# A graph network layer: the first product in one 16-bit pass per tile, with 30 moving nodes

## The chip, the core and the metric

The kernel runs on one core of a Trainium2 chip. The metric is the device time of one execution in microseconds (us), the median of several runs. A core has five engines with queues of their own: TensorE (matmuls; PE in the profile, its weight loads PEld), VectorE (DVE), ScalarE (ACT), GpSimd (POOL) and SyncE (SP), which here only issues transfers. Transfers run on 16 DMA engines.

## The reference

N = 6250 nodes with H = 128 features, E = 100000 edges sorted by destination, four attributes an edge. What is computed, cut to what matters:

```python
src, dst = edge_index                       # dst is sorted
msg_in = concat([x[src], x[dst], edge_attr], axis=1)      # E x 260
h = silu(msg_in @ mW1 + mb1)                              # E x 128
messages = h @ mW2 + mb2
aggregated = segment_sum(messages, dst, num_segments=N)   # N x 128
u = silu(concat([x, aggregated], axis=1) @ uW1 + ub1)
updated = u @ uW2 + ub2
x1 = layer_norm(x + updated, ln_g, ln_b)
out = layernorm(x + x1)
```

Inputs and outputs are float32.

## The kernel before

**Splitting mW1.** `msg_in @ mW1` is the sum of three terms: A[src], with A = x @ mW1[:128]; B[dst], with B = x @ mW1[128:256] + mb1; and the attributes times the last four rows, We. A and B are made once per node (`make_a`, `make_b`) and written to the tables tab_a and tab_b in DRAM. A row of A is fetched for every edge; B, as dst is sorted, is needed only for a short range of nodes at a time.

**Tiles and groups.** An edge tile is 128 edges, a group is G = 8 tiles, so there are NG = 98 groups. Every fifth group from 15 to 90 (16 groups, `by_sort`) does without gathers: A of its edges is selected by 16-bit products with 0/1 matrices (`select`, tile po). The other 82 groups are `listed`; for each, POOL issues eight indirect transfers (`fetch`, line 234, tile ga), of 128 rows each.

**A listed group** goes through these steps:

- `load` (lines 578 to 585), on SP's queue: near, the group's 1024 destinations broadcast to 80 partitions (line 435, 320 KB); mv[:80], 80 consecutive rows of B from the group's first destination on (line 584, 40 KB); and the group's attributes into rows 80 to 83 of st (line 585). We lies in rows 80 to 83 of mv for good.
- `matrices`, on VectorE: st[:80] is the 0/1 matrix "edge e has node base + p" (line 593, a comparison whose accumulator also gives each node's count of edges); oh is the same matrix with the edges on the partitions, 80 columns for each tile (line 603).
- `before_rows`, on TensorE: pre = st.T @ mv, for each tile 128 edges by 128 features, which is B[dst] plus the attributes' term. Everything is float32.
- `hidden`: VectorE adds pre to the gathered rows (line 645), ScalarE takes SiLU (line 646) into h.
- `sums`, on TensorE: pt += h.T @ oh over the eight tiles, so 128 features by 80 nodes, with oh padded to WS = 112 columns. The counts of four groups are transposed together at every fourth group.
- `add`, on VectorE: pt into acc at the group's offset (line 692) and the counts into deg (line 686).

mW2 is merged with uW1, so acc and deg feed the node work directly (`node_u`, `node_y`, `node_z`, `node_o`, once per batch of four node tiles).

**Order.** The order is written out by hand: one stage per listed group g, in which the engines get, in this order, attributes, work on a sorted group, the gathers of the fourth listed group ahead, `load` of the third, `matrices` of the second, `before_rows` and `hidden` of the next, then `sums` and `add` of g, then the rest of the sorted work and the node work (`node_stage`, where `make_b` of later batches ends the stage). Each engine takes its instructions in that order. Every second gather also waits for a product some three stages back, chosen by a running count of TensorE's work (`counted`, with a `share` for cheap products).

**Buffers.** pre has two PSUM buffers (`wide`), which alternate; pt (`narrow`), pn (`bank`) and po (`selected`) have one each. There are four buffers for mv, three for st, two for near.

**Opening and guard.** Before the stages, `tables` turns x, makes A for all nodes and B for the first batches, and prepares lists; the sorting for the 16 groups runs on VectorE during the first stages. Range checks over the indices end in `bad_i`; a slow general path follows only if it is set.

Of the kernel before, what the change touches and what calls it, by code (L numbers as in the profile page):

```python
# [21 lines left out]
P = 128  # L22
# [5 lines left out]
def kernel(  # L28
# [28 lines left out]
    W = 80  # L57
    WS = 112
    NW = NP + W
    AW = 768  # L60
    K1 = W + ED
# [146 lines left out]
    w_row_i = first.tile([P, W], I32, name="w_row_i")  # L208
    nc.gpsimd.iota(w_row_i, pattern=[[1, W]], base=0, channel_multiplier=0)
# [13 lines left out]
    tab_b = dram.tile([NW, H], F32, name="tab_b")  # L223
    sd = dram.tile([4, QN * GE], F16, name="sd")
    ea_d = dram.tile([ED, NG * GE], F32, name="ea_d")
# [3 lines left out]
    def fetch(g):  # L229
# [20 lines left out]
        ceil_i, pattern=[[BN * P, NB + 1], [0, G]], base=BN * P - W, channel_multiplier=0  # L250
    )
    pos_i = first.tile([R, P], I32, name="pos_i")
# [9 lines left out]
    if rest:  # L262
        nc.vector.memset(dst_l[low:NG], N)
    nc.sync.dma_start(dst_l[:low], dst[: low * GE].rearrange("(p j) -> p j", j=GE))
# [9 lines left out]
    w_row = ps1.tile([P, W], F32, name="w_row")  # L274
# [17 lines left out]
    deg_s = []  # L292
    for k in range(3):
        deg_s.append(consts.tile([W, P], F32, name=f"deg_s{k}"))
        nc.vector.memset(deg_s[k], 0.0)

    def deg_at(g):
        s, i = divmod(g - 1, 4) if g else (-1, 0)
        return deg_s[(s + 1) % 3], 32 * i

    def deg_col(g):
        t, c = deg_at(g)
        return t[:, c : c + 1]
# [19 lines left out]
    def lists_1():  # L323
        base_c = first.tile([NG, 1], F32, name="base_c")
        nc.vector.tensor_copy(base_c, dst_l[:, 0:1])
        rel_n = first.tile([P, GE], F32, name="rel_n")[:NG]
        nc.vector.tensor_scalar(rel_n, dst_l, base_c, None, op0=OP.subtract)
        parts.update(base_c=base_c, rel_n=rel_n)
        nc.vector.memset(floor_i[:, 0:1], 0)
        nc.vector.memset(floor_i[:, last[NB - 2] + 1 :], batches[NB - 1][0] * P)  # L330
        nc.vector.memset(ceil_i[:, 84 + G // 2 :], batches[NB - 1][0] * P - W)
        nc.vector.memset(ceil_i[:, 92 + G // 2 :], NP)
        for g in range(NG):
            k = made_for(g)
            usual = (g + G // 2) // G
            if k < usual and g >= G:
                nc.vector.memset(
                    ceil_i[:, g + G // 2 : g + G // 2 + 1],
                    sum(n for _, n in batches[: k + 1]) * P - W,
                )  # L340

    def lists_2():
# [12 lines left out]
        nc.vector.tensor_copy(base_f, to_row(parts["base_c"], NG))  # L355
        parts["base_f"] = base_f

    def lists_3():
# [3 lines left out]
        nc.vector.tensor_scalar(base_p, p_b[:, :NG], p_col, None, op0=OP.add)  # L362
# [6 lines left out]
        nc.vector.tensor_tensor(base_i, base_f, lim, op=OP.min)  # L369
# [12 lines left out]
    mid = (W - 1) / 2  # L382

    def check_1():
        parts["far"] = first.tile([NG, 2], F32, name="far")
        nc.vector.tensor_reduce(parts["far"][:, 0:1], parts["rel_n"], AX.X, OP.max)

    def check_2():
        far = parts["far"]
        nc.vector.tensor_reduce(far[:, 1:2], parts["rel_n"], AX.X, OP.min)  # L390
# [33 lines left out]
    def attribute_rows(c):  # L424
        t = turn.tile([EQ, ED, EJ], F32, name="ea_t")
        nc.scalar.copy(t, ea_l.pop(c).rearrange("q (j d) -> q d j", d=ED))
        to = ea_d[:, c * EC : (c + 1) * EC]
        nc.scalar.dma_start(to.rearrange("d (q j) -> q d j", q=EQ), t)

    def destinations(g):  # L430
        near[g] = work.tile([P, GE], I32, name="near")[:W]
        n = min(GE, E - g * GE)
        if n < GE:
            nc.vector.memset(near[g][:, n:], N)
        nc.sync.dma_start(
            near[g][:, :n],
            dst[g * GE : g * GE + n].rearrange("(o e) -> o e", o=1).to_broadcast([W, n]),
        )
# [18 lines left out]
    def make_b(k):  # L457
        i0, n = batches[k]
        pm = bank()
        product(k, 1, pm)  # L460
        tb = node.tile([P, BN, H], F32, name="o")
        nc.vector.tensor_add(tb[:, :n], pm[:, :n], b1[:, None, :].to_broadcast([P, n, H]))
        nc.sync.dma_start(by_node(tab_b)[:, i0 : i0 + n, :], tb[:, :n])
# [33 lines left out]
    for k in range(NM):  # L497
        mv.append(consts.tile([P, H], F32, name=f"mv{k}"))

    def fill_mv(t):  # L500
        nc.vector.memset(t[P // 2 :], 0.0)
        nc.sync.dma_start(t[W:K1], mW1[2 * H :])

    def fill_ends():
        zeros = first.tile([W, H], F32, name="zeros")
        nc.vector.memset(zeros, 0.0)
        nc.sync.dma_start(tab_b[NP:NW], zeros)
        pad = first.tile([ED, NG * GE - E], F32, name="pad")
# [42 lines left out]
    for k in range(NST):  # L551
        stbuf.append(consts.tile([P, GE], F32, name=f"st{k}"))
    ohbuf = []
    for k in range(NST + 1):
        ohbuf.append(kept.tile([P, G, WS], F32, name=f"oh{k}"))

    fills = [lambda t=t: fill_mv(t) for t in mv] + [fill_ends]
    fills += [lambda t=t: nc.vector.memset(t[:, :, W:], 0.0) for t in ohbuf]
    fills += [lambda t=t: nc.vector.memset(t[P // 2 :], 0.0) for t in stbuf]
# [6 lines left out]
    def load_bases(g):  # L566
        for to, of, eng, top in ((bases, base_i, ENG.SP, NP), (offs, off_i, ENG.DVE, AW - W)):
# [10 lines left out]
    def load(g):  # L578
# [5 lines left out]
        nc.sync.dma_start(mv[turn_of(g) % NM][:W], tab_b[bass.ds(bases[g], W), :])  # L584
        nc.sync.dma_start(stbuf[turn_of(g) % NST][W:K1], ea_d[:, g * GE : (g + 1) * GE])

    oh, pre, xg, h_s = {}, {}, {}, {}

    def matrices(g):
        if g >= NG:  # L590
            return
        n = tiles_of(g)
# [927 lines left out]
```

## Time and profile before

| | |
|---|---|
| median of 3 runs | 1078.12 us (1074.33 to 1084.27) |
| profiled execution, its own time | 1078.25 us |
| span of the profile | 1076.5 us |
| mean granted TensorE clock | 0.863 |
| first gather starts / last gather starts | 4.93 / 1045.23 us |
| 205 to 1045 us: TensorE busy, granted clock | 664.5 of 840 us, 0.89 |
| the same stretch: VectorE, ScalarE, GpSimd busy | 424.7, 341.0, 511.8 us |
| DMA moved | 108.94 MB, of it near 81 x 320 KB, mv 82 x 40 KB, st 82 x 16 KB |

How to read it: a line of a group gives the line of the source, engine, operation, output<-inputs, shape and count; then, after the first bar, the busy time in us and the mean of one in ns; after the second, the idle time of the engine just before them and what ended it. The chain of waits is followed back from the last instruction; its shares say which work set the end. Line 148 is the helper that records every matmul, so products are told apart by their tiles.

### The profile page before, as it was taken

To read this page: it belongs to the slowest core of one execution; us is meant where nothing else is said; L and a number is where in the kernel's file an instruction comes from. 1 tells how busy PE (TensorE), PEld (TensorE's weight loads), DVE (VectorE), ACT (ScalarE), POOL (GpSimd) and SP (SyncE) were. 2 spreads that over 40 slices of the span, in tenths; PEclk is the share of its full clock that TensorE was granted. 3 is DMA by queue.
4 is the path that set the end of the run, shared out by engine and by line. 5 is a ranking of instruction groups with operands and counts; after the bars stand their busy time and mean duration, and the time that the engine had idled before them with its cause. 6 is when DMAs were issued, how large, how long until landed. Compare 5 with 4: busy or idle time off the path is not lost.

```text
span 1076.5 us, 17905 instructions
## 1 busy us (share of the span) xinstructions
PE 807.8 (75%) x6479; PEld 687.8 (64%) x6479; DVE 558.1 (52%) x1357; ACT 404.1 (38%) x543; POOL 641.9 (60%) x665
## 2 busy tenths in 40 slices
PE   5548557668878788877877878777878877877874
PEld 4548455566757576666776666666577666676653
DVE  3463677843555283555373555444374445473282
ACT  1122114533343354344344353343253344363142
POOL 6646557765656666565666566556566566666550
PEclk8778779789888989798998989879879788999795
DMA  9544315342424252525163443424343434242220
GB/s 231 140 114 117 93 57 143 87 101 81 114 85 116 72 137 76 121 75 131 57 152 84 117 109 97 110 80 100 87 112 93 99 92 120 71 111 81 85 77 25
DMA packets 86890, 108.94 MB, mean 101 GB/s; under 512 B 22348, under 2 KB 63456, under 8 KB 86794
## 3 DMA queue, kind: packets, MB, share of 16 engines
q1 hardware_dynamic: 52498, 58.26, 21.3%
q0 software_dynamic: 20928, 42.90, 15.2%
q10 hardware_dynamic: 13368, 6.56, 2.3%
q8 instruction: 53, 0.87, 0.4%
q14 instruction: 43, 0.35, 0.1%
HBM read 96.26 MB, written 11.40 MB: 100 GB/s over the span
## 4 chain that ended last, share of the span: by engine, by line
PE 52%; issue 16%; DVE 13%; another core or an unknown queue 7%; ACT 5%; DMA 3%; POOL 2%; SPq 1%; DVEq 0%; ACTq 0%; POOLq 0%
PE pt L148 14%; PE po L148 14%; PE pre L148 13%; PE pn L148 8%; PE pn L151 2%; POOL ga L234 2%; DMA ga<-tab_a,src_i 1%; DVE st L593 1%; DVE oh L603 1%; ACT h L646 1%; DVE ga L645 1%; ACT O L1027 1%; PE pre L151 1%; DVE O L1023 1%
## 5 line engine op out<-in xcount | busy, mean ns | idle before, releaser
L234 POOL DMA_INDIRECT ga<-tab_a,src_i x614 | 601.9, 980 | 380.4 <-issue 202.4
L148 PE MATMUL pre<-mv,st 128*128 128x128 f32 x1308 | 202.3, 310 | 27.4 <-issue 12.8
L148 PEld LDWEIGHTS pre<-mv,st 128*128 128x128 f32 x1308 | 190.5, 225 | 40.3 <-issue 29.2
L148 PE MATMUL pt<-oh,h 128*128 128x112 f32 x1308 | 191.5, 305 | 25.6 <-issue 12.6
L148 PEld LDWEIGHTS pt<-oh,h 128*128 128x128 f32 x1308 | 180.1, 218 | 39.5 <-issue 24.3
L646 ACT ACTIVATE h<-ga 128x1024 f32<-128x1024 f32 (+1 forms) x78 | 81.1, 1042 | 317.7 <-DVE ga L645 222.6
L692 DVE TENSOR_TENSOR acc<-acc,pt 128x80 f32 x98 | 23.3, 238 | 341.3 <-PE pt L148 104.1
L148 PE MATMUL po<-O,A_low 128*128 128x157 bf16 (+47 forms) x896 | 163.8, 225 | 22.3 <-issue 22.3
L148 PE MATMUL po<-O,A 128*128 128x156 bf16 (+37 forms) x1376 | 140.2, 227 | 36.6 <-issue 33.0
L148 PEld LDWEIGHTS <-A 128*128 128x128 bf16 x1376 | 112.4, 104 | 58.3 <-issue 57.3
L645 DVE TENSOR_TENSOR ga<-ga,pre 128x1024 f32<-128x1024 f32 (+1 forms) x78 | 93.3, 1197 | 54.7 <-PE po L148 22.0
L593 DVE TENSOR_SCALAR_CACHE_REDUCE st<-near,base_p 80x1024 f32<-80x1024 int32 x82 | 103.4, 1261 | 11.9 <-issue 10.4
L148 PEld LDWEIGHTS <-A_low 128*128 128x128 bf16 x896 | 91.0, 103 | 20.6 <-issue 20.3
L1027 ACT ACTIVATE O<-sc,p_less 128x512 bf16<-128x512 f16 x128 | 84.8, 711 | 1.4 <-DMA sc<-sd 1.4
L1028 ACT ACTIVATE O<-O,ones 128x1024 bf16<-128x1024 bf16 x64 | 73.5, 1148 | 2.1
L603 DVE TENSOR_TENSOR oh<-w_row,rel 128x640 f32<-128x640 f32 x82 | 66.9, 816 | 0.8
L151 PE MATMUL pn<-ident,hT 128*128 128x128 f32 x128 | 23.2, 310 | 45.1 <-issue 10.2
L1070 ACT ACTIVATE hT<-po 128x512 f32<-128x512 f32 x32 | 19.0, 593 | 91.4 <-PE po L148 51.7
L234 POOL DMA_INDIRECT ga<-in_x_dram,src_i x40 | 38.3, 959 | 23.2 <-issue 9.9
L151 PEld LDWEIGHTS pn<-ident,hT 128*128 128x128 f32 x128 | 15.5, 154 | 51.1 <-issue 24.3
L148 PE MATMUL pt<-oh,h_s 128*128 128x112 f32 x256 | 34.8, 290 | 12.6 <-ACT h_s L1079 7.9
L148 PE MATMUL pn<-Oc,at_s 128*128 128x512 f32 x64 | 37.8, 675 | 8.0 <-issue 5.6
(221 smaller groups left out, 921.9 us busy)
## 6 DMA issues: line engine op xcount, KB each, us to landing
near<-in_dst_dram SPq DMA_DIRECT2D x81, 320.0 KB
ga<-tab_a,src_i POOLq DMA_INDIRECT x614
sc<-sd SPq DMA_DIRECT2D x16, 512.0 KB
mv<-tab_b SPq DMA_DIRECT2D x82, 40.0 KB
tab_a<-A SPq DMA_DIRECT2D x11, 256.0 KB
tab_b<-o SPq DMA_DIRECT2D x11, 256.0 KB
out_dram<-o ACTq DMA_DIRECT2D x11, 256.0 KB
x<-in_x_dram SPq DMA_DIRECT2D x10, 256.0 KB
```

The lines of the kernel that those rows point to most:

```text
L148: counted(nc.tensor.matmul(to, *operands, **flags), to, share)
L151: counted(nc.tensor.transpose(to, *operands), to)
L234: ins = nc.gpsimd.indirect_dma_start(out=rows[g][:, i, :], out_offset=None, in_=x if g < RAW else tab_a[:, :], in_offset=bass.IndirectOffs ...
L593: nc.vector.tensor_scalar(stbuf[turn_of(g) % NST][:W], near.pop(g), base_p[:W, g : g + 1], 0.0, op0=OP.is_equal, op1=OP.add, accum_out=deg ...
L603: nc.vector.tensor_tensor(oh[g][:, :n, :W], w_row[:, None, :].to_broadcast([P, n, W]), rel[:, g, :n, None].to_broadcast([P, n, W]), op=OP. ...
L645: nc.vector.tensor_add(s[:, i], s[:, i], p[:, i])
L646: nc.scalar.activation(h[:, i], s[:, i], AF.Silu)
L692: nc.vector.tensor_add(to, to, pt[:, :W])
L1023: nc.vector.tensor_scalar(O[:, j], key, p_rows[:, r : r + 1], None, op0=OP.is_equal)
L1027: nc.scalar.activation(O[:, j], key, AF.Square, bias=p_less[:, r : r + 1])
L1028: nc.scalar.activation(O[:, 2:], O[:, 2:], AF.Relu, bias=ones[:, 0:1], scale=-1.0)
L1070: nc.scalar.activation(now["hT", half], now.pop("po"), AF.Silu)
```

## The change

The first product is made in 16 bit. B and the attributes are each cut into three bfloat16 parts whose sum is the float32 value (high, middle, low). A tile no longer has all of the group's nodes: tile i of a group gets V = 30 nodes, from node base + 8 i on, where the base is now a multiple of S = 8 and chosen from the group's middle edge. Its rows are 3 x 30 = 90 for B and 9 x 4 = 36 for the attributes (each part of We with each part of the attributes), 126 in all, so one bfloat16 pass takes the place of the float32 product.

- B's parts go to a table tab_p, laid out so that for each of the 30 rows the eight tiles' nodes are one run of 2 KB; mv becomes [128, 8, 128] bfloat16, filled by four transfers a group. tab_b stays for the sorted groups.
- near becomes the edge's offset inside its tile (float16, from off_d), on 90 partitions; st is a bfloat16 comparison with `third`, which is the partition's number divided by three, with no accumulator.
- oh has VS = 32 columns a tile, and each tile's product in `sums` adds to 32 of the 88 columns of pt, shifted by 8 a tile; a first product with zeros (`none`) clears pt.
- The counts come from products of ones with oh (`degrees`), four a group, and are added to deg in every group.
- Making B's parts and the attributes' parts takes several steps on several engines; each chain of steps is spread over one stage by `go_on`, and its PSUM tile comes from `wide`.
- In the count of work for the gathers, the products of pre and of the counts have a share of 1/4.

```diff
-    W = 80
-    WS = 112
+    S = 8
+    V, VS = 30, 32
+    W = S * (G - 1) + VS
+    F = 2 * S
+    D = W // S
...
-    K1 = W + ED
+    KB, K1 = 3 * V, 3 * V + 9 * ED
...
+    tab_p = dram.tile([S, 3, ND, H], BF16, name="tab_p")
+    off_d = dram.tile([NG, GE], F16, name="off_d")
+    we_d = dram.tile([9 * ED, G * H], BF16, name="we_d")
...
-    def attribute_rows(c):
-        t = turn.tile([EQ, ED, EJ], F32, name="ea_t")
-        nc.scalar.copy(t, ea_l.pop(c).rearrange("q (j d) -> q d j", d=ED))
-        to = ea_d[:, c * EC : (c + 1) * EC]
-        nc.scalar.dma_start(to.rearrange("d (q j) -> q d j", q=EQ), t)
+    def attribute_steps(c, pm):
+        v = pm[:EQ, : ED * EJ].rearrange("q (d j) -> q d j", d=ED)
+        t = turn.tile([EQ, 3, ED, EJ], BF16, name="ea_t")
+
+        def high():
+            nc.scalar.copy(v, ea_l.pop(c).rearrange("q (j d) -> q d j", d=ED))
+            nc.scalar.copy(t[:, 0], v)
+
+        def middle():
+            nc.vector.tensor_sub(v, v, t[:, 0])
+            nc.scalar.copy(t[:, 1], v)
+
+        def low():
+            nc.vector.tensor_sub(t[:, 2], v, t[:, 1])
+            nc.scalar.dma_start(
+                ea_d[:, c * EC : (c + 1) * EC].rearrange("r (q j) -> q r j", q=EQ),
+                t.rearrange("q s d j -> q (s d) j"),
+            )
+
+        return [high, middle, low]
 
     def destinations(g):
-        near[g] = work.tile([P, GE], I32, name="near")[:W]
...
+        near[g] = work.tile([P, GE], F16, name="near")[:KB]
+        nc.sync.dma_start(near[g], off_d[g : g + 1, :].to_broadcast([KB, GE]))
...
-    def make_b(k):
+    def b_steps(k, pm):
         i0, n = batches[k]
-        pm = bank()
-        product(k, 1, pm)
-        tb = node.tile([P, BN, H], F32, name="o")
-        nc.vector.tensor_add(tb[:, :n], pm[:, :n], b1[:, None, :].to_broadcast([P, n, H]))
-        nc.sync.dma_start(by_node(tab_b)[:, i0 : i0 + n, :], tb[:, :n])
+        m = P * n // BN
+        v = pm[:m]
+        t = node.tile([P, BN, 3, H], BF16, name="tb", bufs=1)[:m]
+
+        def begin():
+            for i in range(BN):
+                matmul(
+                    pm[:m, i, :], xT[k][:, i : n * P : BN], w1[:, 1, :], start=True, stop=True
+                )
+
+        def high():
+            nc.vector.tensor_add(v, v, b1[:m, None, :].to_broadcast([m, BN, H]))
+            nc.scalar.copy(t[:, :, 0], v)
+            tb = node.tile([P, BN, H], F32, name="o")[:m]
+            nc.scalar.copy(tb, v)
...
+        def middle():
+            nc.vector.tensor_sub(v, v, t[:, :, 0])
+            nc.scalar.copy(t[:, :, 1], v)
+
+        def low():
+            nc.vector.tensor_sub(t[:, :, 2], v, t[:, :, 1])
+            d0 = (i0 * P + F) // S
+            for u in range(S // BN):
+                nc.sync.dma_start(
...
@@ load
-        nc.sync.dma_start(mv[turn_of(g) % NM][:W], tab_b[bass.ds(bases[g], W), :])
-        nc.sync.dma_start(stbuf[turn_of(g) % NST][W:K1], ea_d[:, g * GE : (g + 1) * GE])
+        to = mv[turn_of(g) % NM].rearrange("r i f -> r (i f)")
+        for a in range(D - G + 1):
+            n = min(S, V - a * S)
+            nc.sync.dma_start(
+                to[3 * S * a : 3 * S * a + 3 * n],
+                tab_p[:n, :, bass.ds(bases[g] + a, G), :].rearrange("b s d f -> (b s) (d f)"),
+            )
+        cols = slice(g * GE, (g + 1) * GE)
+        nc.sync.dma_start(
+            stbuf[turn_of(g) % NST][KB:K1],
+            ea_d[:, cols].rearrange("(o r) e -> o r e", o=1).to_broadcast([3, 3 * ED, GE]),
+        )
@@ matrices
-            stbuf[turn_of(g) % NST][:W],
-            near.pop(g),
-            base_p[:W, g : g + 1],
-            0.0,
-            op0=OP.is_equal,
-            op1=OP.add,
-            accum_out=deg_col(g),
+            stbuf[turn_of(g) % NST][:KB], near.pop(g), third[:KB], None, op0=OP.is_equal
         )
...
@@ before_rows
-                pre[g][:, i, :], st[:, i, :], mv[turn_of(g) % NM], start=True, stop=not raw
+                pre[g][:, i, :], st[:K1, i, :], mv[turn_of(g) % NM][:K1, i, :],
+                start=True, stop=not raw, share=1 / 4,
             )
@@ sums
+    def degrees(g, to):
+        if g in by_sort:
+            transpose(to, deg_s[by_sort[g] % 2], ident[:W, :W])
+            return
+        o = oh[g]
+        for a in range(D - G + 1):
+            n = D if a == 0 else G
+            matmul(
+                to[:, a * S : (a + n) * S], ones[:, 0:1], o[:, :n, a * S : (a + 1) * S],
+                start=a == 0, stop=a == D - G, share=1 / 4,
+            )
...
-        for i in range(n):
-            matmul(
-                pt[:, :WS], h[:, i, :], o[:, i, :], start=i == 0, stop=i == n - 1
-            )
+            matmul(pt[:, :W], none[:, :P], none[:, P:], start=True, stop=False, share=1 / 4)
+            for i in range(n):
+                matmul(
+                    pt[:, i * S : i * S + VS], h[:, i, :], o[:, i, :],
+                    start=False, stop=i == n - 1,
+                )
@@ the stages
+        chain = []
+        for k in range(2, NB):
+            if j == x_stage(k) + 2:
+                chain = b_steps(k, wide()[:, :BN])
...
+                chain = [None] + attribute_steps(c, wide().rearrange("p i f -> p (i f)"))
+        chain = iter(chain)
...
         matrices(ahead(g, 2))
+        go_on()
...
         hidden(ahead(g, 1))
+        go_on()
...
         add(g, sums(g))
+        go_on()
```

Left out: the lists and range checks recomputed for the new windows, the filling of the new tables with zeros and with We's parts, the offset F = 16 of acc and deg, the sorted groups' own 0/1 matrix of 88 columns, and the general path's reading of the new tables.

## The prediction

> **What bounds the kernel now.** I read the engine totals and the chain of waits first, then the costliest groups, then the timeline of a middle stretch to get the pitch of the products, and last the table by stretches for the clock.
>
> ```profile
> PE 807.8 (75%) x6479; PEld 687.8 (64%) x6479; DVE 558.1 (52%) x1357; ACT 404.1 (38%) x543; POOL 641.9 (60%) x665
> PE 52%; issue 16%; DVE 13%; another core or an unknown queue 7%; ACT 5%; DMA 3%; POOL 2%; SPq 1%; DVEq 0%; ACTq 0%; POOLq 0%
> PE pt L148 14%; PE po L148 14%; PE pre L148 13%; PE pn L148 8%; PE pn L151 2%; POOL ga L234 2%; DMA ga<-tab_a,src_i 1%; DVE st L593 1%; DVE oh L603 1%; ACT h L646 1%; DVE ga L645 1%; ACT O L1027 1%; PE pre L151 1%; DVE O L1023 1%
> ```
>
> TensorE is the busiest engine and carries half of the chain. The two products that the change touches are 13% (pre, the first product) and 14% (pt, the sums) of it: 140 and 151 us of the span of 1076.5. The 16% "issue" is TensorE standing with nothing visible to wait for; this change does not address it.
>
> ```profile
> L234 POOL DMA_INDIRECT ga<-tab_a,src_i x614 | 601.9, 980 | 380.4 <-issue 202.4
> L148 PE MATMUL pre<-mv,st 128*128 128x128 f32 x1308 | 202.3, 310 | 27.4 <-issue 12.8
> L148 PE MATMUL pt<-oh,h 128*128 128x112 f32 x1308 | 191.5, 305 | 25.6 <-issue 12.6
> L593 DVE TENSOR_SCALAR_CACHE_REDUCE st<-near,base_p 80x1024 f32<-80x1024 int32 x82 | 103.4, 1261 | 11.9 <-issue 10.4
> L603 DVE TENSOR_TENSOR oh<-w_row,rel 128x640 f32<-128x640 f32 x82 | 66.9, 816 | 0.8
> L692 DVE TENSOR_TENSOR acc<-acc,pt 128x80 f32 x98 | 23.3, 238 | 341.3 <-PE pt L148 104.1
> ```
>
> 654 tiles stand as 1308 matmuls: one float32 product is two passes. The means of 310 and 305 ns overlap each other, so a pitch is read from the chain and the timeline instead:
>
> ```profile
> 596.84 1.79 PE pre L148 x16
> 598.62 1.77 PE pt L148 x16
> 600.40 0.89 PE pn L148 x2
> ```
> ```profile
> 613.54 0.21 PE L148 MATMUL po<-O,A_low 128*128 128x103 bf16 x1
> ...
> 613.70 0.22 PE L148 MATMUL po<-O,A_low 128*128 128x131 bf16 x1
> ...
> 613.88 0.22 PE L148 MATMUL po<-O,A_low 128*128 128x135 bf16 x1
> ```
>
> A pass of pre (128 columns) takes 1.79/16 = 0.112 us, one of pt (112 columns) 1.77/16 = 0.111, one of 512 columns 0.89/2 = 0.445. Between two A_low lines lie three 16-bit matmuls: 0.16/3 = 0.053 us up to 131 columns, 0.18/3 = 0.060 up to 135. So 128 columns in one pass: 0.057 us.
>
> **The change part by part**
>
> First product. 654 tiles x 2 x 0.112 = 146 us become 654 x 0.057 = 37. Of the 140 us on the chain a quarter stays (0.46/1.79 of a group): 140 - 36 = **-104**.
>
> Sums' columns, 112 to 32. Here the row decides. 128 and 112 columns have the same pitch (0.112, 0.111), so columns are not the limit. [...] I take **0**, as the two equal pitches say, and keep -100 as the other end. Nothing in this trace moves 32 float32 columns.
>
> Degrees. The comparison's accumulator goes; per group four float32 products with one stationary column take its place, over 88 + 3 x 64 = 280 columns in two passes. At 0.445/512 us a column: 0.49 us a group. TensorE's time on pt is on the chain for 151 of 98 x 1.77 = 173 us, 87%: 82 x 0.49 x 0.87 = **+35**. The clearing product `none` (16 bit, 88 columns, near 0.045 us) is 82 x 0.045 x 0.87 = **+3**. The transposes of the counts go from 26 to 16: -1.
>
> VectorE, groups listed. st: 1.261 + 0.078 for the accumulator become one 16-bit comparison over 1024 columns. The nearest row is O<-sc,p_rows (128x512 bf16 from f16, 0.360): between 0.36 and 0.72; I take 0.6, saving 0.74. oh: 640 to 256 columns; the add over 1024 takes 1.214 and this one over 640 0.818, so 1.03 ns a column and 0.42 left, saving 0.40. Together 82 x 1.14 = 93 us of busy time, but most of it is cover: st and oh are on the chain for 1% each, about 11 us each, of which 11 x 0.74/1.34 + 11 x 0.40/0.82 = **-11**. The degree add stays one a group (0.23); it was four in a row, every fourth group.
>
> Tables. B in three parts and the attributes in three parts run as a chain of steps spread over a stage, in 11 + 9 stages. VectorE gets two subtractions of 512 columns (0.69, row o<-pn,b): 20 x 1.38 = 28 us; a quarter of VectorE's busy time is on the chain (140 of 558): **+7**. ScalarE gets three copies of 0.58 in 11 stages and about 0.7 us more in 9: 25 us, of which 5% x 1076/404 = 13% is on the chain: **+3**. In the opening, two B chains and one attribute chain run at once, each with two handovers between VectorE and ScalarE: 3 x 2 = **+6**.
>
> The chain's PSUM tile. It comes from the two buffers in which pre alternates and is held from the stage's start to the last subtraction, which stands in VectorE's queue behind the adds of acc and deg. So the next stage's pre waits for 0.24 + 0.23 + 0.69 = 1.16 us after the sums end, unless TensorE has node work there: 20 x 1 = **+20**. Who waits for that: everything in TensorE's queue, sorted work too. Bounds: 0 (always covered) and 110 (rival D).
>
> Transfers. Per group near falls from 80 rows of 4 KB to 90 of 2 KB, mv grows from 40 KB in one issue to 180 KB in four, the attributes from 16 to 72 KB: 376 to 432 KB, 5 MB over the run, against 108.9 MB moved at about 40% DMA share. SP issues six transfers a group instead of three, each about 0.33: 1 us more in a stage of some 10; the writes of B's parts (two a batch, 256 byte runs) and three-part attributes pass the same queues. Counted 0: loads lead by three stages. If that lead were used up, 82 us from SP's issues alone, and every load behind them late. The same lead covers mv's wait for the later write of tab_p.
>
> Sum: -104 + 0 + 35 + 3 - 1 - 11 + 7 + 3 + 6 + 20 = -42. The profiled execution took 1078.25 us (span 1076.5), as good as the median of 1078.12: 1078 - 42 = 1036.
>
> **The clock.** The rows by stretches of 20 us from 205 to 1045: where TensorE was busy under 75% (11 stretches) the mean granted clock was 0.87, at 80 to 90% (19 stretches) 0.88. [...] The rows show no such slope: I take 0.
>
> **The rivals**
>
> A, as summed: 1036.
>
> B, more comes out. For: both dense engines get shorter, and the sums may follow their columns. What stands next is POOL: 654 gathers at a pitch of 1.25 us (0.95 and 0.30 idle between two in the timeline) are 818 us; with 5 us before the first and 31 after the last starts, 854. At 1036 this is not yet the bound, but each wait of a gather for a product shrinks only as products do. [...]
>
> C, the freed time becomes waits. For: 28% of the chain is issue, unknown, DMA and POOL, and none of that shrinks; TensorE's instructions stay about 6550 (654 fewer, 738 more) while they go by faster, so stalls at "issue" may take back what the passes gave. Then 1060 to 1085, near 1072.
>
> D, slower, by one mechanism: the chain's tile in pre's two buffers. The middle subtraction stands in VectorE's queue behind the add of the next group's gathered rows. Where ScalarE now waits for gathers, it is 47.1 us in 12 times, 3.9 each; today TensorE works past such a lateness because pre of the next group has a buffer. With the tile held, pre waits for rows that it doesn't need: 3.9 + 1.16, near 5.5 us with the handovers, in 20 stages: 110 in place of 20, 1036 + 90 = 1126. It decides from about 3.7 us a stage (20 x 2.7 more is +54). Against: few of the 82 stages show late rows now. [...]
>
> That the change doesn't do what it says holds for one part only, the columns of the sums, and is counted at 0.
>
> **How the numbers follow.** A 0.50, B 0.13, C 0.15, D with the clock 0.22. A change within 1% (1067 to 1089) can't be told from none here. A is faster in 0.46 and the same in 0.04; B faster; C 0.03, 0.08, 0.04; D slower but for 0.01. Together faster 0.62, same 0.13, slower 0.25. The predicted time is A's, 1036. A's own range is 1000 to 1070 (path share, 0 to 40 us for the held tile). For 8 in 10 it reaches down to B at 975 and up to 1105, leaving out the deep end of B (0.06) and the upper half of D (0.11).
>
> **What would show it.** Right: pre as 654 bf16 matmuls, eight in about 0.46 us in the timeline; eight float32 tiles of the sums still near 1.75 us for 16 passes with weight loads end to end; st near 0.6 and oh near 0.42; pre under 5% of the chain; about one us of TensorE waiting for VectorE at pre after a chain's stage. Wrong: pt passes well under 0.1 us (B); unchanged spans between groups with more "issue" (C); pre's idle time charged to VectorE for over 60 us, or a steady clock below 0.82 (D). An opening much over 120 us to the last raw group, or SP's loads arriving late before st or pre, would say that the transfers were not hidden.

## The result, and the profile after

The changed kernel takes 1146.24 us (median of 4 runs, 1144.65 to 1147.55), the kernel before 1079.28 beside it: a ratio of 1.062 (95% interval 1.0567 to 1.0672). It is slower by some 67 us, where 42 less were forecast, and outside the range of 975 to 1105.

The page of the changed kernel: totals by engine, the granted clock in 40 slices, the chain of waits by engine and by line, and the groups of the dense products.

```profile
PE 878.4 (77%) x6558; PEld 696.3 (61%) x6558; DVE 481.1 (42%) x1330; ACT 433.4 (38%) x602; POOL 658.2 (57%) x667
...
PEclk9877655677777667687777778777677687877755
...
PE 61%; issue 14%; DVE 7%; ACT 4%; another core or an unknown queue 3%; DMA 1%; SPq 1%; DVEq 0%; ACTq 0%; POOL 0%; POOLq 0%
PE pt L152 23%; PE po L152 17%; PE pn L152 11%; PE pre L152 7%; PE pn L155 2%; ACT O L1141 1%; DVE O L1137 1%; DMA at_s<-in_edge_attr_dram 1%; DMA mv<-tab_p 1%; ACT O L1142 1%; DVE deg L798 1%; DVE ga L740 1%; SPq L678 0%; DVE st_s L1153 0%
...
L152 PE MATMUL pt<-oh,h 128*128 128x32 f32 x1308 | 207.4, 316 | 16.4 <-issue 16.3
...
L152 PE MATMUL pre<-mv,st 126*128 126x128 bf16 x654 | 79.1, 277 | 19.4 <-issue 7.5
...
L152 PE MATMUL pn<-Oc,at_s 128*128 128x512 f32 x64 | 51.0, 892 | 3.8 <-issue 3.8
```

Start at the end. The product pn<-Oc,at_s is touched by nothing in the change: 64 passes of 512 columns in both kernels. In the kernel before its line is

```profile
L148 PE MATMUL pn<-Oc,at_s 128*128 128x512 f32 x64 | 37.8, 675 | 8.0 <-issue 5.6 <-DVE st_s L1039 2.4
```

Its mean was 675 ns and is 892, the same work in a third more time. The clock goes with it: the mean granted clock over the whole span is 0.725 and was 0.863; over these 64 passes alone it is 0.72 and was 0.92. The same can be seen in the chain. po, the selecting products of the sorted groups, had 14% of 1076.5 and has 17% of 1145: 151 and 195 us. pn in this line went from 8 to 11%, 86 to 126 us. Some 84 us came onto the chain at products that compute what they computed before.

By stretches of the changed kernel (columns: the stretch; busy time of TensorE, its weight loads, VectorE, ScalarE, GpSimd with their instructions; granted clock; DMA share; GB/s):

```profile
205.00:1100.00 895.00, 721.17 (x5714) 567.22 (x5714) 368.86 (x949) 366.98 (x509) 530.36 (x528) 0.74 0.39 103
```

The kernel before was busy on TensorE for 664.5 of 840 us, 79%, at a clock of 0.89; here it is 81% at 0.74. So TensorE is no less busy, and the clock still fell. Nor is there more idle time: between 205 and 1045 us neither a matmul nor a weight load runs for 170 us before and 161 us after; the stretches of over 3 us are 11 of together 43 us before, 7 of 30 us after.

Two groups in the timeline of the changed kernel (start, duration, then the work; x16 are the 16 passes of a group's sums):

```profile
589.55 3.62 PE L152 MATMUL pt<-oh,h 128*128 128x32 f32 x16
...
645.02 1.97 PE L152 MATMUL pt<-oh,h 128*128 128x32 f32 x16
```

and, in the timeline of the kernel before, the sums of a sorted group, which have 112 columns there:

```profile
598.46 1.94 PE L148 MATMUL pt<-oh,h_s 128*128 128x112 f32 x16
```

At full clock 32 columns take what 112 took (1.97 and 1.94 us). The other group takes nearly twice as long. The stretches around those two groups say why; the first number after GpSimd's count is the granted clock, 0.50 and 1.00:

```profile
588.42:593.17 4.75, 4.75 (x27) 4.41 (x27) 0.76 (x1) 2.62 (x4) 2.31 (x3) 0.50 0.67 190
644.37:646.99 2.62, 2.62 (x27) 2.45 (x27) 0.76 (x1) 1.17 (x2) 1.89 (x2) 1.00 0.44 138
```

TensorE was busy without a break in both: 4.75 of 4.75 us, and 2.62 of 2.62.

Where the prediction had named signs, the groups with forms kept apart show:

```profile
L152 PE MATMUL pre<-mv,st 126*128 126x128 bf16 x654 | 79.1, 277 | 19.4 <-issue 7.5 <-DMA mv<-tab_p 7.0 <-DVE deg L798 1.9
...
L693 DVE TENSOR_SCALAR st<-near,third 90x1024 bf16<-90x1024 f16 x82 | 39.4, 481 | 17.7 <-issue 17.7
...
L697 DVE TENSOR_TENSOR oh<-w_row,rel 128x256 f32<-128x256 f32 x82 | 33.7, 411 | 0.5
```

654 one-pass products, st at 0.48 us, oh at 0.41, and the line names 1.9 us in which TensorE stood at pre for VectorE. In the chain eight passes of pre take 0.45 us in some groups and 0.85 in others:

```profile
582.82 0.45 PE pre L152 x8
...
639.97 0.85 PE pre L152 x8
```

### The profile page after: what moved, and what is told of

The parts are those of the page before. It is cut to its first block, busy times and chain, and to the rows that moved or that the text cites. A ratio compares the mean times of both kernels' runs of the same rounds, so it can differ in the third digit from the quotient of the medians.

```text
span 1145.0 us, 19046 instructions
## 1 busy us (share of the span) xinstructions
PE 878.4 (77%) x6558; PEld 696.3 (61%) x6558; DVE 481.1 (42%) x1330; ACT 433.4 (38%) x602; POOL 658.2 (57%) x667
## 2 busy tenths in 40 slices
DMA packets 115306, 120.44 MB, mean 105 GB/s; under 512 B 50535, under 2 KB 79103, under 8 KB 115203
## 4 chain that ended last, share of the span: by engine, by line
PE 61%; issue 14%; DVE 7%; ACT 4%; another core or an unknown queue 3%; DMA 1%; SPq 1%; DVEq 0%; ACTq 0%; POOL 0%; POOLq 0%
PE pt L152 23%; PE po L152 17%; PE pn L152 11%; PE pre L152 7%; PE pn L155 2%; ACT O L1141 1%; DVE O L1137 1%; DMA at_s<-in_edge_attr_dram 1%; DMA mv<-tab_p 1%; ACT O L1142 1%; DVE deg L798 1%; DVE ga L740 1%; SPq L678 0%; DVE st_s L1153 0%
## 5 line engine op out<-in xcount | busy, mean ns | idle before, releaser
L152 PE MATMUL pt<-oh,h 128*128 128x32 f32 x1308 | 207.4, 316 | 16.4 <-issue 16.3
L152 PEld LDWEIGHTS pt<-oh,h 128*128 128x128 f32 x1308 | 197.3, 236 | 24.0 <-issue 19.0
L803 DVE TENSOR_TENSOR acc<-acc,pt 128x88 f32 x98 | 24.0, 245 | 442.5 <-PE pt L152 215.2
L152 PE MATMUL pre<-mv,st 126*128 126x128 bf16 x654 | 79.1, 277 | 19.4 <-issue 7.5
L152 PEld LDWEIGHTS <-st 126*128 126x128 bf16 x654 | 64.9, 132 | 37.6 <-issue 32.9
L152 PE MATMUL pt<-oh,ones 128*1 128x64 f32 (+1 forms) x648 | 67.7, 255 | 24.6 <-issue 10.8
L152 PEld LDWEIGHTS pt<-oh,ones 128*1 128x1 f32 x648 | 46.5, 94 | 54.7 <-issue 31.0
L152 PE MATMUL pt<-oh_s,h_s 128*128 128x88 f32 x256 | 49.1, 365 | 23.4 <-ACT h_s L1193 18.6
L152 PEld LDWEIGHTS pt<-oh_s,h_s 128*128 128x128 f32 x256 | 46.4, 276 | 24.7 <-ACT h_s L1193 19.4
L152 PE MATMUL pre<-w,xT 128*128 128x128 f32 (+2 forms) x186 | 43.4, 406 | 17.3 <-ACT xT L483 8.7
```

What stands on the lines that cost most here:

```text
L152: counted(nc.tensor.matmul(to, *operands, **flags), to, share)
L803: nc.vector.tensor_add(to, to, pt[:, :W])
```

## The experiments

The two theories at the start: **the clock** (the narrow sums let TensorE's clock fall, though they take as long at full clock), and against it **the added work** (steps of the three parts, counts, transfers, the opening). A third question ran beside: what the first product is worth alone.

One thing about the numbers. The kernel before took 1071 to 1079 us in some sittings and 890 to 893 in others, on the same code. So every run is compared with runs of before in its own sitting, and each table row below names that time. The clock in the last column is that of the run whose profile was kept; the runs of before had 0.89 to 0.92 in the sittings near 890 and 0.85 to 0.87 in those near 1072.

| run | before beside it | time | ratio (95%) | clock in the profile |
|---|---|---|---|---|
| the change | 1079.28 | 1146.24 | 1.062 (1.0567 to 1.0672) | 0.725 |
| e1_pad128: change, sums 128 columns | 889.90 | 920.41 | 1.0364 (1.032 to 1.0407) | 0.892 |
| e1b_pad64: change, sums 64 columns | 889.90 | 941.88 to 966.49 | none given | 0.815 |
| e2_narrow: before, 7 of 8 tiles' sums 32 columns | 889.90 | 911.98 | 1.0278 (1.0218 to 1.0337) | 0.850 |
| e4_pre16: before, first product one pass | 889.90 | 880.55 | 0.9914 (0.9877 to 0.9951) | 0.862 |
| c_after: the change | 892.51 | 965.34 | 1.0794 (1.0738 to 1.085) | 0.786 |
| c_pad128: as e1_pad128 | 892.51 | 928.82 | 1.0362 (1.0291 to 1.0434) | 0.888 |
| e5_one_count: change, one count product | 892.51 | 962.14 | 1.0685 (1.0572 to 1.0798) | 0.759 |
| e6_one_part: change, one part only | 892.51 | 935.27 | 1.0457 (1.0404 to 1.0511) | 0.809 |
| f1_pad_opening: 128 columns, lighter opening | 1071.40 | 1104.17 | 1.0316 (1.0247 to 1.0384) | 0.840 |
| f2_pre16_128: e4 with 128 columns | 1071.40 | 1064.30 | 0.9941 (0.9916 to 0.9966) | 0.833 |
| f3_pad_one_part: 128 columns, one part | 1071.40 | 1091.24 | 1.0224 (1.0134 to 1.0313) | 0.849 |
| g1_pre16_pace: f2, gathers paced at 4.5 | 892.11 | 878.58 | 0.9843 (0.977 to 0.9916) | 0.866 |
| g2_pad_one_one: f3, one count product | 892.11 | 894.95 | 1.004 (1.0009 to 1.0071) | 0.880 |
| g3_pad_one_pace: f3, gathers paced at 4.5 | 892.11 | 893.70 | 1.0017 (0.9996 to 1.0039) | 0.910 |
| g4_before_pace: before, gathers paced at 4.5 | 892.11 | 895.10 | 1.0033 (0.999 to 1.0075) | 0.893 |
| h1_one_part: f3 again | 1071.72 | 1094.33 | 1.0201 (1.0133 to 1.0268) | 0.845 |
| h2_one_count: g2 again | 1071.72 | 1087.14 | 1.0131 (1.0052 to 1.021) | 0.829 |
| h3_pace: g3 again | 1071.72 | 1107.09 | 1.0368 (1.0286 to 1.045) | 0.837 |

**The same sums with more columns.** Each 0/1 matrix of 32 columns is moved four times in one pass, into four places of pt of which only the first is read. The weights and the number of passes stay; the clear grows from 88 to 352 columns and pt's buffer from 256 to 512 columns.

```diff
-            matmul(pt[:, :W], none[:, :P], none[:, P:], start=True, stop=False, share=1 / 4)
+            matmul(pt[:, : TIMES * W], none[:, :P], none[:, P:], start=True, stop=False, share=1 / 4)
...
-                    pt[:, i * S : i * S + VS], h[:, i, :], o[:, i, :],
+                    pt[:, : TIMES * W].rearrange("p (r c) -> p r c", c=W)[
+                        :, :, i * S : i * S + VS
+                    ],
+                    h[:, i, :],
+                    o[:, i, None, :].to_broadcast([P, TIMES, VS]),
```

TIMES is 4 in e1_pad128 and 2 in e1b_pad64. In the same sitting, 32 columns were put into before's sums, so that the narrowing stands alone (the nodes of seven tiles beyond the first 32 are left out of the sums):

```diff
-                pt[:, :WS], h[:, i, :], o[:, i, :], start=i == 0, stop=i == n - 1
+                pt[:, : WS if i == 0 or g in by_sort else 32],
+                h[:, i, :],
+                o[:, i, : WS if i == 0 or g in by_sort else 32],
+                start=i == 0, stop=i == n - 1,
```

> The changed kernel with one thing added: each product of the sums moves its 32 columns four times, into four places of pt of which only the first is read, so 128 columns stream through the array in a pass that its weight load makes 0.11 us long anyway; the clearing product grows from 88 to 352 columns. Theory 1 (the granted clock follows the columns that are streamed): mean clock 0.72 goes back to 0.84 or more, and the time falls from 1146 to 1020 to 1075 us. Theory 2 (the time went into waits: the held PSUM tile, the count products, the transfers): more work and nothing taken away, so clock 0.72 and 1150 to 1160 us. Theory 3 (the clock fell because TensorE has more idle time): TensorE's busy time is the same, so clock 0.72 and 1150 us.

> The same with two copies, 64 columns a pass. Theory 1: between the two, clock 0.76 to 0.82 and 1080 to 1130 us. Theories 2 and 3: as the changed kernel, 1146 to 1155 us and clock 0.72.

> The kernel before, with the columns of the listed groups' sums cut from 112 to 32 in seven of the eight tiles (it leaves out the sums of nodes 32 to 79 there); nothing else changes. Theory 1: the clock falls from 0.86 to 0.78 or less and the time rises by 30 to 80 us, although nothing is added. Theories 2 and 3: the pass is bound by its weight load, so 1070 to 1082 us and clock 0.86.

Narrowing alone makes the kernel before slower, by 2.8%, though it only takes work away: its four runs have a clock of 0.85 to 0.87, those of before beside it 0.90 to 0.92. That is the plainest single result of the study. With 64 columns the changed kernel takes 942 to 966 us, too wide a spread for a ratio, with 128 columns 920. As the change itself was not in this sitting, the pair was run again with it:

> The changed kernel, beside its variants on one chip. Theory 1 (the clock follows the streamed columns): lowest clock of the four here bar none, 0.72 to 0.78, and 6% or more slower than before, more than that where gathers set the pace of before. Theory 2 (waits): the same 6%, clock not what sets it.

> The changed kernel with the sums' columns moved four times, again, on the same chip as the changed kernel. Theory 1: 60 to 120 us less than the changed kernel, clock 0.10 to 0.17 higher. Theory 2: 5 to 15 us more than the changed kernel.

965.34 became 928.82: 37 us come back when TensorE is given four times the columns to stream. Theory 1 had the direction in all these runs and expected too much: 60 to 120 us here, and for e2_narrow 30 to 80 us with a clock of 0.78 or less, where 22 us and 0.85 were measured. The pages of the two, c_after first:

```profile
PE 787.5 (81%) x6558; PEld 635.7 (66%) x6558; DVE 482.6 (50%) x1330; ACT 432.4 (45%) x602; POOL 651.1 (67%) x667
...
PEclk9868955588879587969798889877868897878755
...
PE 54%; DMA 11%; ACT 10%; DVE 8%; issue 5%; POOL 2%; SPq 1%; DVEq 0%; ACTq 0%; POOLq 0%
```
```profile
PE 728.0 (78%) x6558; PEld 589.4 (63%) x6558; DVE 482.6 (52%) x1330; ACT 432.2 (46%) x602; POOL 660.4 (71%) x667
...
PEclk9975996799999799999989789989888888989987
...
PE 46%; DMA 13%; ACT 10%; DVE 8%; issue 7%; POOL 7%; SPq 0%; DVEq 0%; ACTq 0%; POOLq 0%
```

The number of matmuls is the same to the last one (6558), and TensorE's busy time falls by 60 us as the clock rises from 0.786 to 0.888. On the chain TensorE loses more than the kernel gains: 54% of 968 is 523 us, 46% of 930 is 428. Of these 95 us some 60 turn into waits for transfers, GpSimd and issue, so the clock's price for the whole is smaller than its price for TensorE. The padding costs little at full clock, as its timeline shows beside the 1.97 us above; the clear, over 352 columns now, grew from 0.21 to 0.32. Together that is 0.19 us a group, 16 us over 82 groups if all of it were on the chain (an estimate):

```profile
568.20 0.32 PE L153 MATMUL pt<-none 1*128 1x352 bf16 x1
568.44 2.05 PE L153 MATMUL pt<-oh,h 128*128 128x128 f32 x16
```

**The first product alone.** Before, with st, mv, B and the attributes in bfloat16 (one part, so B and the attributes are rounded), with a cast of We and a second table's writes added in the opening, all else as before; f2_pre16_128 also has WS = 128 in place of 112.

```diff
-        nc.sync.dma_start(mv[turn_of(g) % NM][:W], tab_b[bass.ds(bases[g], W), :])
+        nc.sync.dma_start(mv[turn_of(g) % NM][:W], tab_b16[bass.ds(bases[g], W), :])
...
-                pre[g][:, i, :], st[:, i, :], mv[turn_of(g) % NM], start=True, stop=not raw
+                pre[g][:, i, :], st[:, i, :], mv[turn_of(g) % NM], start=True, stop=not raw,
+                share=1 / 4,
```

> The kernel before, with the first product alone in one 16-bit pass: B and the attributes rounded to 16 bits (their middle and low parts are left out), sums of 112 columns, counts by the accumulator and the PSUM tile of make_b as before. The chain's first product goes from 140 to about 36 us. Theory 1: 112-column sums keep most of the streaming, clock 0.78 to 0.84, 1000 to 1050 us. Theory 2 (the other parts of the change cost what it lost): clock near 0.86 and 970 to 1000 us. Theory 3 (idle time): clock 0.75 or less, 1050 us or more.

> The kernel before with the first product in one 16-bit pass (B and the attributes rounded to 16 bits, their middle and low parts left out) and the sums' padding raised from 112 to 128 columns. Theory 1 (clock by streamed columns): clock 0.87 or more against 0.86 with 112 columns; where before takes 890 us the gathers' pitch (654 x 1.25 us and both ends, 854) leaves little: 865 to 882 us, ratio 0.975 to 0.99; where before takes 1078 us, 960 to 1020. The other theories: as with 112 columns, ratio 0.99.

0.9914 and 0.9941: the removal of 654 passes, priced at -104, gives 6 to 9 us. The two sittings show two different reasons. In the one where before takes 890, GpSimd stands next. The busy tenths of GpSimd over the span of e4_pre16, and the list of its gathers (duration, then first and last start):

```profile
POOL 5577778777777777777777777777777777777770
```
```profile
L235 POOL DMA_INDIRECT ga<-tab_a,src_i x614: 940/944/3471, 65.5 to 855.8; - x154
```

There is no hole anywhere in the row. 613 distances between gathers in 790 us are 1.289 each, against the 1.25 of gathers that follow without a wait; with all 654 at 1.25 and the 36 us of the ends the floor is 854. That is 36 us under before, so TensorE's passes could give no more than this there, and gave 9. Some of the rest probably went in the opening: the first gather from tab_a starts at 65.5 us, and at 56.6 in e2_narrow, which has before's opening and ran in the same sitting. In the sitting where before takes 1071 there are holes. f2_pre16_128:

```profile
PE 721.7 (68%) x5825; PEld 588.7 (55%) x5825; DVE 556.6 (52%) x1358; ACT 410.3 (38%) x556; POOL 638.8 (60%) x665
...
PE 41%; issue 14%; DVE 11%; another core or an unknown queue 7%; ACT 5%; DMA 3%; SPq 1%; POOL 1%; DVEq 0%; ACTq 0%; POOLq 0%
```

TensorE is busy for 86 us less than in the first profile of before (807.8), and its share of the chain falls from 52 to 41%; from 205 to 1045 us the time in which neither a matmul nor a weight load runs rises from 170 to 239 us. ScalarE's idle time ahead of h that ends with a gather's landing rises with it:

```profile
L659 ACT ACTIVATE h<-ga 128x1024 f32<-128x1024 f32 x76 | 80.3, 1056 | 270.4 <-DVE ga L658 163.1 <-DMA ga<-tab_a,src_i 72.8 <-issue 34.5
```

```profile
L646 ACT ACTIVATE h<-ga 128x1024 f32<-128x1024 f32 x76 | 80.3, 1057 | 317.7 <-DVE ga L645 222.6 <-issue 47.8 <-DMA ga<-tab_a,src_i 47.1
```

It was 47.1, in the second of these lines, and is 72.8. Most of the freed time is waiting again; late gathers are the part of it that the profile names, and what delays them in these sittings stays open. Two other things took a part that no run separates. The clock fell here too: 0.82 to 0.84 in the runs of f2_pre16_128 against 0.85 to 0.87 of before, and 0.86 to 0.87 in those of e4_pre16 against 0.90 to 0.92. On the 41% of the chain that TensorE has in f2_pre16_128, 438 us, the fall from 0.865 to 0.833 is some 16 us (an estimate). And its first gather from tab_a starts at 75 us, where before has 69.

**The parts, the counts and the opening.** e5_one_count leaves three of the four count products out (the counts of most nodes are then missing). e6_one_part leaves out the middle and the low part of B and of the attributes: zeros stand in their rows, both subtractions of each chain go, with one copy for B and two for the attributes, and the attributes' chain holds no PSUM tile.

```diff
-        for a in range(D - G + 1):
-            n = D if a == 0 else G
+        for a in range(1):
+            n = D
```
```diff
-        def middle():
-            nc.vector.tensor_sub(v, v, t[:, :, 0])
-            nc.scalar.copy(t[:, :, 1], v)
...
-            nc.vector.tensor_sub(t[:, :, 2], v, t[:, :, 1])
```

> The changed kernel with one of the four count products a group (it leaves out the counts of the other three: 280 columns become 88). By the prediction's own sum the three are 24 us of the chain. Theory 1: the three stream densely, so without them the clock falls a little and at most 20 us come back, possibly none. Theory 2: 25 to 40 us come back, clock the same.

> The changed kernel with B and the attributes in one 16-bit part (it leaves out the middle and low parts, whose places stay zero): the two subtractions and the copies go, the chain's PSUM tile is free after the first copies in place of the stage's end; transfers and products are the same. By the prediction's sum 7 + 3 + 6 + 20 = 36 us come back. Theory 1: under 20 us come back, the clock stays under 0.78. Theory 2 (rival D of the prediction, the held tile): 60 us or more come back.

One count product in place of four: 3 us less, with intervals that overlap, so nothing that can be told from none. Its clock is lower (0.759 against 0.786), as the text for theory 1 had it, so part of what came back may have been lost to the clock. One part: 30 us less, between what the two theories expected. Its clock is a little higher too (0.809), so a few of these 30 may be the clock's.

The next run combined 128 columns with an opening in which the load of We is issued first, and the writes of We's parts and of the tables' zeros go on ScalarE's queue in place of SP's; and 128 columns with one part.

```diff
+    we_first = first.tile([ED, H], F32, name="we")
+    nc.scalar.dma_start(we_first, mW1[2 * H :])
...
-                nc.sync.dma_start(
+                nc.scalar.dma_start(
```

> The changed kernel with the sums' columns moved four times and a lighter opening: We's load goes first on ScalarE's queue instead of ahead of a waiting VectorE cast, and the nine writes of its parts and the seven writes of zeros go through ScalarE's queue instead of SP's. In the changed kernel's trace the cast waits 5 us for that load and the sixteen issues hold SP's queue for 10.6 us. If that is the opening's cost, gather 40 starts 8 to 15 us earlier than with the columns alone (79 to 82 us there) and the time is that much less, 910 to 920 us on a chip where before takes 890, still above it; if the opening is hidden by what follows, nothing comes back.

> The changed kernel with the sums' columns moved four times and B and the attributes in one 16-bit part (middle and low left out). With the narrow columns the parts' chains were worth 30 us. If they cost by the held tile and the queues, the same 25 to 35 us come back from the 928 us of the wide columns; if they cost mostly in the opening, 10 to 15 us come back, all before gather 40.

The reason given for the slower opening fell. The first gather from tab_a starts at 69 us before and 82 after, and with the lighter opening still at 81. With one part it starts at 77 here, and at 69 in e6_one_part, where c_after beside it has 80. So the parts' steps hold at least some of it up, and SP's queue none that shows. Near 890 the distance is wider: 80 in c_after, 56 to 57 in e2_narrow and g4_before_pace. As for the time, f3_pad_one_part takes 10 us less than f1_pad_opening by the ratios (1.0224 and 1.0316) and 13 by the medians; that is what the parts cost with wide sums.

**What is left with 128 columns and one part.** A slow pace of the gathers was the theory: every second gather waits for a product chosen by the count of work, and PACE = 4.5 in place of 3.5 lets it start a stage earlier.

```diff
-    PACE = 3.5
+    PACE = 4.5
```

> The first product alone in one 16-bit pass (rounded parts, sums of 128 columns), with the gathers allowed one stage earlier (PACE 4.5 in place of 3.5). Theory P (the first product's gain is held back because each gather waits for a product 3.5 stages back): ratio to before falls from 0.994 to 0.97 or less. Theory Q (the gain goes into other waits of TensorE): ratio 0.985 to 1.0.

> The changed kernel with wide sums and one part (both as before), and one of the four count products a group (the other counts left out). By the prediction the three products are 24 us of the chain; with a clock that is held up by the wide sums they should now show: ratio from 1.022 to 1.00 to 1.005. If count products lie beside other work, the ratio stays at 1.02.

> The changed kernel with wide sums, one part and PACE 4.5. Theory P: ratio from 1.022 to 1.00 or less. Theory Q: 1.01 to 1.03.

> The kernel before with PACE 4.5, as the control for the two others: if the pace is no bound there, ratio 0.99 to 1.01; if it is a bound of its own, under 0.99, and the gains of the others are measured against this.

In this sitting (before at 892) GpSimd's rows in the other three are nearly without holes too, and all three lie within 0.4% of before; only g1_pre16_pace beats before, at 0.9843, with B and the attributes rounded to one part. The kernel with wide sums, one part, four counts and PACE 3.5 was not run near 890, so what the count or the pace alone gives there is not known. For the sittings near 1072 the set was run once more, with it:

> The changed kernel with wide sums and one part (middle and low left out), PACE 3.5 and all four count products: the common ground of the two runs beside it, on one chip with them. Where gathers' pitch bounds before (890 us): ratio 1.010 to 1.025; where before takes 1075 us: 1.015 to 1.03.

> The same with one of the four count products (the counts of the other three are left out). If the three cost what the prediction gave them, 15 to 25 us less than the run with all four; if they lie beside other work, within 8 us of it.

> The same as the first with PACE 4.5. If the gathers' pace holds the gain (theory P): 15 us or more below the first; if not, within 8 us of it.

One count product in place of four gives 7 us there (1094.33 to 1087.14, intervals that overlap). The pace theory falls: with 4.5 the kernel is slower, 1107.09.

## Why the prediction was wrong

Two steps failed. By size the larger is the first product, "A quarter stays: -104", which alone gave 6 to 9 us: with that one term corrected the prediction's sum goes from -42 to about +55. The other is the clock, counted at 0, which cost 33 to 37 us: corrected alone it leaves about -7. Terms that were counted too high, the counts and the parts, hid a part of the two. The clock is the step whose cause the runs show, so it comes first.

"The rows show no such slope: I take 0." This compared stretches of 20 us by TensorE's busy time, and found 0.87 and 0.88. Busy time counts a pass that waits for its weights, and the change left just that: passes that take 0.11 us with 32 columns as with 112 or 128 (16 in 1.97, 1.94 and 2.05 us above) and stream for a small part of it. The 16 weight loads fill 1.86 of the 1.97 us and 1.87 of the 1.94, end to end. A float32 column of a pass is counted here as 0.87 ns, from the 0.445 us that a pass of 512 takes in the prediction's chain of before, and a 16-bit column as half of it, as 135 of them took 0.060 us there, both at a granted clock of 1.00. This is an estimate. So 112 columns stream for 97 of the 111 ns of a pass, and 32 for 28. To see whether that decides, the traces of all 20 profiles were cut into the steps in which the granted clock changes, 3.413 us; it has two values there, 1.0 and 0.5. For each step, the time that its streamed columns take at full clock (0.87 ns for a float32 column, half of it for a 16-bit one) as a share of the step, and the mean clock of the step after it:

| streamed share of a step | steps | mean clock of the next step |
|---|---|---|
| under 0.21 | 720 | 0.50 |
| 0.21 to 0.31 | 428 | 0.51 |
| 0.31 to 0.35 | 210 | 0.53 |
| 0.35 to 0.38 | 152 | 0.58 |
| 0.38 to 0.40 | 217 | 0.66 |
| 0.40 to 0.42 | 128 | 0.78 |
| 0.42 to 0.46 | 410 | 0.91 |
| 0.46 to 0.52 | 530 | 0.98 |
| over 0.52 | 2827 | 0.99 |

In these traces one threshold, 0.40, tells the next step's clock in 5265 of 5622, 94%. The best threshold on the share of the step in which a matmul ran tells it in 83%, and the clock of the step itself in 71%. Of the steps in which matmuls ran for 99% or more, those above 0.40 were followed by full clock in 96% of cases, those below in 20%. A step of nothing but 32-column passes has 28/111 = 0.25, in a row with 0.51 after it; one of 112 columns has 0.88, in the row with 0.99. Over the span the mean share is 0.57 before and 0.39 after; in the pair of one sitting it is 0.47 with 32 columns (c_after) and 0.62 with 128 (c_pad128). The table is a regularity of the traces; that the columns move the clock, and not the other way round, is what c_pad128 (0.888 for 0.786) and e2_narrow (0.85 to 0.87 for 0.90 to 0.92) show, since they change columns and, but for the wider clear, nothing else. In the prediction's D stands a slower clock too, with no run that shows its size or its cause; what the runs showed in its place is a clock that went from 0.89 to 0.74 between 205 and 1045 us, while the time with neither a matmul nor a weight load went from 170 to 161 us.

Point by point, by the prediction's terms:

- **First product, -104.** The passes went as said (8 in 0.45 us at full clock), but the term was read as a share of the chain, and alone it gives 6 to 9 us. "A quarter stays: -104" passes over what stands next. Rival B had named the gathers' pitch of 1.25 us and taken it as a bound for a faster kernel only; where before takes 890 us it binds at once. Rival C (waits in place of passes) is what f2_pre16_128 shows near 1071, beside a lower clock and a later opening that it had not named.
- **Sums' columns, 0.** Right for the pass, 1.97 us for 16 with 32 columns against 1.94 with 112. The other end of -100, and B's 975 with it, is shown by no run: the narrowing alone took 22 us more (e2_narrow). Wrong for the kernel: by the clock they cost 37 us near 892 (c_after less c_pad128) and about 33 near 1072 (1.062 less 1.0316, from two sittings), with the padding's own cost, at most 16 us, on the other side.
- **Counts, +35.** The three products that e5 and h2 leave out were 24 of it, and measured 3 and 7 us, neither clear of the noise. That they lie beside other work is the likely reading; the lower clock without them (0.759 for 0.786, 0.829 for 0.845) may hide a part.
- **The parts' chains, +7, +3, +6 and +20 for the held tile.** 36 in sum; 30 were measured by e6_one_part, 10 to 13 with wide sums (f1 to f3). The single terms were off: the first gather from tab_a starts 13 us later and not 6, and the held tile cost little at pre (1.9 us of waiting for VectorE). Rival D, the slower case, had the sign right by a mechanism that did not occur; of its signs the clock below 0.82 did come, for another reason.
- **st and oh, -11.** st took 0.481 where 0.6 was assumed, oh 0.411 for 0.42; the saving is real (VectorE 77 us less busy) and mostly hidden, as said.
- **Transfers, 0.** TensorE waited 7.0 us for mv at pre; not far from hidden. 120.44 MB were moved, 11.5 more, where 5 were counted: those were the groups' loads alone, without the writes of the new tables.

In ratios, from the sittings where before takes 1071 to 1079: 1.062 for the change, 1.032 with 128 columns (and the lighter opening, which moved no gather), 1.020 to 1.022 with one part as well, 1.013 with one count product too. The first product alone is 0.994. Each has an interval of 0.3 to 0.9% to both sides. The distance from 1.013 to 0.994, about 20 us, is not settled: the clears, the four transfers for mv, the counts that remain and the rest of the opening were not taken out one by one.

## What to carry to other kernels

Price a dense product twice: by the time of its pass, and by the columns that it streams in that time. Here a product bound by its weights with few columns (1.86 of 1.97 us are weight loads) kept TensorE busy and let its clock fall (0.863 to 0.725), and every other product paid; columns added under the weight load cost little (2.05 for 1.97 us) and held the clock (0.888 for 0.786). And before a share of the chain is counted as a gain, work out the floor of the engine that stands next, here the gathers' pitch: 13% of the chain was worth under 1%, and 1.6% with the gathers let go earlier.

## What was not expected of the hardware

- That leaving work out of TensorE, and nothing else, makes the kernel slower (e2_narrow, 1.0278).
- That one threshold of streamed columns, 0.40 of a 3.413 us step by the count above, tells the clock of the next step in 94% of 5622 steps.
- That one program takes 890 us in one sitting and 1072 in another, even on the same chip (892.11 and 1071.72), with a clock of 0.89 to 0.92 against 0.85 to 0.87. How an edit ranks depends on it: the kernel with wide sums, one part and PACE 4.5 is level with before near 892 (1.0017) and 3.7% slower near 1072 (1.0368). What makes the two stays open. The traces show where they differ: in all eight profiles of the slower sittings 35 to 42 of GpSimd's waits ahead of a gather, 50 to 60 us, are put down to another core or an unknown queue, and all engines stand still together for over 0.5 us 21 to 32 times; in the twelve others there is no such wait, and 1 to 3 such halts.
